# A transformer block on one core: weight parts spread over the heads, and a written order for VectorE and ScalarE in the FFN

## The chip, the cores and the metric

The kernel runs on one core of a Trainium2 chip. The metric is the device time of that core in microseconds (us), the median of several runs of the compiled program. The engines are called as in the profile: PE is TensorE, DVE is VectorE, ACT is ScalarE, POOL is GpSimd, and SP is SyncE, which issues the DMAs.

## The reference

For B=4 batches of S=512 tokens with D=256 features, everything in fp32:

```python
sa, ca, ga, sb, cb, gb = (silu(c) @ wmod).reshape(B, 6, 1, D) parts
ga, gb = sign * max(|g|, 0.25)
h = layernorm(x) * (1 + ca) + sa
x = x + ga * attention(h)          # 16 heads of 128, causal softmax, W_O
h = layernorm(x) * (1 + cb) + sb
x = x + gb * ffn(h)

def ffn(x):
    h = x @ down_w + down_b                      # 256 -> 128
    logits = x @ router_w + router_b - 1e-7 * cost
    top 2 of softmax(logits); gate = softmax of the two
    out = sum over the two of gate * expert(h * mask) summed over all 8 experts
          # expert: gelu(gelu(hm) @ w1 + b1) @ w2 + b2, hidden 128, 256, 384, 512 (twice)
    out += 0.1 * shared_expert(h)
    return out @ up_w + up_b + gelu(x) @ core_w + core_b
```

## The kernel before

**Products.** Each fp32 product is made of three products of rounded parts (`mm3`, lines 139 to 141): a matrix is split into hi (rounded, a copy on ACT or DVE) and lo (the rest, a subtraction in `rest`, line 147, on DVE or POOL).

**Heads.** The first loop runs over 64 heads: four groups of four heads, in each group over the batches. A head makes its scores (L475 is its first product, a diagonal block), the mask with the row maximum (DVE, L481, which gives `nmax`), the exponentials (ACT, L491), the row sums' reciprocals and a scaling (POOL, L496), a transpose through DRAM (`turned`, tile `aT`), the hi and lo parts of it, the product with the values (`mixed`, tile `pz`, parts `zh` and `zl`) and the product with W_O (`project_out`, tile `po`). At the last head of a batch the residual is added: `tmp` on DVE (L583), `x` on POOL (L585). The products with the values lag `LAG` heads behind.

**Weight units.** The FFN's weights are kept as units of up to 512 columns. Eleven of them (`TO_PART`: first0 to first4, second0 to second2, shared, core, down) are split during the heads by `part_wf`: a load into a buffer of tag "stage" (two buffers), a hi copy on ACT (L227), a store of it to DRAM, the subtraction on POOL, and a store of that. They are loaded again later into the buffers of the weights. Head number n splits the unit that `PART_AT` gives for it.

**FFN.** `all_ffn` runs over 4 batches and in each over 21 chunks of 128 hidden units (k = 0 to 20; the last is the shared expert). `first` makes the chunk's first product `ph` (from `ghh` and `ghl`, the parts of gelu(down)) and its gelu `hid` on ACT; where the chunk is not used whole, ACT and DVE then split it into `ah` and `al`. Three chunks later (`FFN_LAG`) `second` makes the product `acc`, DVE evicts an expert's sum into `part`, and POOL adds it to `oacc` (L856). `gelu_inputs`, called at k=10, makes gelu(x) and its parts for the core product (POOL adds h2F at L864, ACT's gelu, POOL's `gxh` and `gxl`); `core` at k=19 and 20 (`FFN_CORE`) makes that product and `outputs` of a batch comes at k=6 of the next. `output_bias` loads `out_b` and makes `obias` on POOL (L725) at k=12 of batch 0.

**Norm and routing.** The FFN of batch b needs its second layernorm and its routing. `normed` makes statistics on DVE (L346, L348), `rstd` on POOL (L350, L351: an addition and a power) and `xn` on DVE (L354); `modulated` transposes it on PE (`ptn`, L383), scales it, and splits it into `hTh` and `hTl`; `route` makes the router's product (`pl`, L610) and then a chain of short DVE operations on [32 x 128] tiles with three trips to ACT (L642 among them). `finish` enters these steps into `later` for two to eight steps after the batch's last head: for batch 0 and 1 these are still heads (batch 1's modulation and routing fall on heads 62 and 63), for batch 2 and 3 they lie among the chunks of batch 0 and 1, two or three chunks to a step.

**Order.** PE's instructions run in the order of the program from the start (`manual_schedule`, L150). The other engines' instructions are put in order by the scheduler, which works through a simulated timeline, takes the program's order as priority, and lets an instruction that is ready pass one that is not. Some are tied by `issue_after`.

Of the kernel before, what the change touches and what calls it, by code (L numbers as in the profile page):

```python
# [11 lines left out]
F32 = mybir.dt.float32  # L12
# [83 lines left out]
FFN_CORE = (19, 20)  # L96
BEFORE3 = 4
EARLY = 2

TO_PART = tuple(u for u, (_, in_parts) in UNITS.items() if in_parts)  # L100
PART_AT = (17, 19, *range(20, 28), 33)
# [11 lines left out]
def adaln_attention_moe_kernel(  # L113
# [103 lines left out]

    def part_wf(u: str):

        n = len(UNITS[u][0]) * P  # L220
        st = work.tile([P, 512], F32, tag="stage", name=f"st_wf_{u}")[:, :n]
        load_runs(st, wf_runs(u))
        d = parts_d[u] = dram.tile([P, 3, n], F32, tag=f"wfp_{u}", name=f"wfp_{u}")
        if u.startswith("second"):
            nc.sync.dma_start(d[:, 2, :], st)
        hi = work.tile([P, 512], F32R, tag="stage", name=f"hi_wf_{u}")[:, :n]
        nc.scalar.copy(hi, st)  # L227
        nc.sync.dma_start(d[:, 0, :], f32(hi))
        rest(nc.gpsimd, st.bitcast(F32R), st, hi)
        nc.sync.dma_start(d[:, 1, :], st)  # L230
# [110 lines left out]
    def normed(b: int, which: int):  # L341

        st = small.tile([P, NT, 6], F32, tag="st", name=f"st_{b}_{which}")
        mv = small.tile([P, NT, 2], F32, tag="mv", name=f"mv_{b}_{which}")
        for t in range(NT):
            nc.vector.bn_stats(st[:, t, :], xs[b][:, t, :])  # L346
        for t in range(NT):
            nc.vector.bn_aggr(mv[:, t, :], st[:, t, :])  # L348
        rstd = small.tile([P, NT], F32, tag="rstd", name=f"rstd_{b}_{which}")
        nc.gpsimd.tensor_scalar(rstd, mv[:, :, 1], LN_EPS, 1.0, ALU.add, ALU.mult)  # L350
        nc.gpsimd.tensor_tensor(rstd, rstd, minus_half, ALU.pow)  # L351
        xn = work.tile([P, DC, NT, P], F32, tag="xn", name=f"xn_{b}_{which}", bufs=1)
        for t in range(NT):
            nc.vector.tensor_scalar(  # L354
                xn[:, :, t, :],
                xs[b][:, t, :].rearrange("p (c d) -> p c d", c=DC),
                mv[:, t, 0:1],
                rstd[:, t : t + 1],
                ALU.subtract,
                ALU.mult,  # L360
            )
        return xn
# [8 lines left out]
    def modulated(b: int, which: int):  # L371


        xn = xns[b, which]
        hi = const.tile([P, DC, S], F32R, tag=f"hTh{b}", name=f"hTh_{b}_{which}")
        lo = const.tile([P, DC, S], F32R, tag=f"hTl{b}", name=f"hTl_{b}_{which}")
        (h2T if which else hT)[b] = hi, lo
        first = not (b or which)
        whole = []
        for c in range(DC):  # L380
            ptr = psum.tile([P, S], F32, tag="pj", name=f"ptn_{b}_{which}_{c}", bufs=3)
            for t in range(NT):
                nc.tensor.transpose(ptr[:, ts(t, P)], xn[:, c, t, :], ident)  # L383
            scale = modT[:, 4 * which + 2 + c, b : b + 1]
# [6 lines left out]
            whole.append(ptr)  # L391

            for d in (c,) if not first else range(DC) if c == DC - 1 else ():
                nc.scalar.copy(hi[:, d, :], whole[d])
                recent["norm"] = rest(nc.vector, lo[:, d, :], whole[d], hi[:, d, :]).ins
            yield
# [4 lines left out]

    def norm_batch(b: int, which: int):
        if which and b > 1:
            with tc.issue_after(recent["hidden"]):
                xns[b, which] = normed(b, which)
            return
        xns[b, which] = normed(b, which)
# [184 lines left out]
    def route(b: int):  # L592

        n = S // R
# [14 lines left out]
        for i, (c, a) in enumerate(parts):  # L609
            nc.tensor.matmul(  # L610
                pl, lhsT=rw[:, c], rhs=a[:, c, :], start=i == 0, stop=i == len(parts) - 1
            )
        lt = work.tile([P, S], F32, tag="stage", name=f"lt_{b}")[:R]
        nc.vector.transpose(lt, pl)
        lt3 = lt.rearrange("p (j e) -> p j e", e=R)
        lg = small.tile([P, n * E], F32, tag="r_lg", name=f"r_lg_{b}", bufs=1)[:R]
# [6 lines left out]
        nc.vector.tensor_tensor(lg, lg, row(rbias[:R]), ALU.add)  # L623
        m, sm, f, g1, g2 = (t2(nm) for nm in ("m", "sm", "f", "g1", "g2"))
        desc = rt[:R, R_DESC - R_ROUTER : R_DESC - R_ROUTER + E]

        def top(hot):


            nc.vector.tensor_reduce(m, lg, AX.X, ALU.max)  # L630
            nc.vector.tensor_tensor(lg, lg, each(m), ALU.subtract)
            nc.vector.scalar_tensor_tensor(s, lg, 0.0, row(desc), op0=ALU.is_ge, op1=ALU.mult)  # L632
            nc.vector.tensor_reduce(f, s, AX.X, ALU.max)
            nc.vector.tensor_tensor(hot, s, each(f), ALU.is_equal)

        def exp(to, a, spare):


            if b == 0:
                last_exps["route"] = nc.scalar.activation(to, a, AF.Exp).ins  # L640
                return
            nc.scalar.activation(to, a, AF.Tanh, scale=0.5)  # L642
            nc.vector.tensor_scalar(spare, to, -1.0, 1.0, ALU.mult, ALU.add)
# [3 lines left out]
        top(hot1)  # L647
        exp(ex, lg, gt)
# [3 lines left out]
        top(gt)  # L652


        exp(g1, m, g2)
        nc.vector.scalar_tensor_tensor(g1, g1, 1.0, sm, op0=ALU.subtract, op1=ALU.mult)
        nc.scalar.activation(g1, g1, AF.Tanh, scale=-0.5)
        nc.vector.tensor_scalar(g2, g1, -0.5, 0.5, ALU.mult, ALU.add)
        nc.vector.tensor_scalar(g1, g1, 0.5, 0.5, ALU.mult, ALU.add)
        nc.vector.tensor_tensor(hot1, hot1, each(g1), ALU.mult)  # L660
        nc.vector.tensor_tensor(gt, gt, each(g2), ALU.mult)

# [66 lines left out]

    def before_chunks(b: int):  # L730
# [18 lines left out]
    class Mixture:  # L749
# [23 lines left out]
        def first(self, k: int, at: int):  # L773
# [14 lines left out]
            if k in WHOLE or (not b and k < NCH):  # L788
                tag = "aTh" if b and WHOLE.index(k) % 3 == 2 else "qh"
                if not b:  # L790
                    tag = ("qh", "e")[k % 2]
                hid = work.tile([P, S], F32, tag=tag, name=f"hid_{b}_{k}")
                recent["hidden"] = nc.scalar.activation(
                    hid, ph, AF.Gelu, bias=bias
                ).ins
                return k, hid
            hid = work.tile([P, S], F32, tag="e", name=f"hid_{b}_{k}")
            nc.scalar.activation(hid, ph, AF.Gelu, bias=bias)
            self.parted += 1
# [3 lines left out]
            if e == E:  # L803
                nc.scalar.activation(ah, hid, AF.Copy, scale=0.1)
                nc.vector.scalar_tensor_tensor(
                    al, hid, 0.1, f32(ah), op0=ALU.mult, op1=ALU.subtract
                )
            else:
                recent["hidden"] = nc.scalar.copy(ah, hid).ins
                recent["parted"] = rest(nc.vector, al, hid, ah).ins  # L810
# [47 lines left out]
        def gelu_inputs(self):  # L858

            hh, hl = h2T[self.b]  # L860
            gxh, gxl = self.gx
            hF = work.tile([P, DC, S], F32, tag="T", name=f"h2F_{self.b}")
            for c in range(DC):
                nc.gpsimd.tensor_tensor(hF[:, c, :], f32(hh[:, c, :]), f32(hl[:, c, :]), ALU.add)  # L864
                nc.scalar.activation(hF[:, c, :], hF[:, c, :], AF.Gelu)
                nc.gpsimd.tensor_scalar(gxh[:, c, :], hF[:, c, :], 1.0, 1.0, ALU.mult, ALU.mult)
                rest(nc.gpsimd, gxl[:, c, :], hF[:, c, :], gxh[:, c, :])
# [53 lines left out]
    def all_ffn():  # L921
# [5 lines left out]
        for b in range(B):  # L927
            m = Mixture(b)
            for k in range(NCH + 1):
# [6 lines left out]
                going.append((m, *begun))  # L936
                at += 1
                if k == FFN_OUT and before:
                    before.outputs()
                if k == 10:  # L940
                    with tc.issue_after(recent["added"]):
                        m.gelu_inputs()
                if at == NCH + FFN_LAG:
# [6 lines left out]
                if b + 1 < B:  # L950
                    if k == 16:
                        prepared[b + 1] = before_chunks(b + 1)
                    if k in FFN_CORE:
                        m.core(len(m.pys))
# [39 lines left out]
    def finish(n: int, b: int, h: int, z):  # L994
        project_out(b, h, z)
        if h == H - 1:
            later.setdefault(n + 1, []).append((norm_batch, b, 1))
            later.setdefault(n + 3 + (b > 1) + (BEFORE3 - 1) * (b > 2), []).append((modulate, b, 1))
            later.setdefault(n + 4 + (b > 1) + (BEFORE3 - 1) * (b > 2), []).append((route, b))
# [21 lines left out]
    for n, (b, h) in enumerate(order):  # L1021
# [18 lines left out]
        for f, *args in later.pop(n, ()):  # L1040
            f(*args)
        if n in PART_AT:
# [42 lines left out]

    steps = all_ffn()
# [6 lines left out]
    while going:  # L1093
# [4 lines left out]
        end_norm()  # L1098
        if waiting:
            db, dh, aT = waiting.pop(0)  # L1100
            done.append((db, dh, mixed(db, dh, aT)))
        if n == N:
            with tc.issue_after(recent["z"]):
                part_one(-1)
# [84 lines left out]
```

## Time and profile before

| | us |
|---|---|
| median of 3 runs | 824.99 (823.43 to 825.74) |
| the profiled execution | 824.06 |
| its span, first to last instruction | 822.3 |
| PE busy in it | 777.1 (95%) |
| DVE, POOL, ACT busy | 597.4, 521.4, 490.4 |
| mean granted clock of PE | 0.988 |
| heads | about 20 to 625 |
| FFN chunks | about 625 to 822 |

The page's busy shares are averages over the heads and the FFN, which have different loads. A line of the timeline gives start, length, engine, line of the code, operation, output and inputs, and in brackets the idle time before it and what ended that. In a line of waits the columns are total, number and longest.

### The profile page before, as it was taken

The page shows a single profiled execution, that of the slowest core. Times are in us where ns is not written, and L with a number is a line of the kernel's source. Part 1 is how long each engine was busy: PE and PEld are TensorE (multiplying, and loading weights), DVE is VectorE, ACT ScalarE, POOL GpSimd, SP SyncE. Part 2 cuts the span into 40 slices and gives each one's busy share as a digit, 9 for nine tenths or more (in the row PEclk, how much of TensorE's full clock was granted, in tenths as well). Part 3 has the DMA queues.
Part 4 walks back from the last instruction along what each step waited for, and adds up shares of the span by engine and source line. Part 5 has one row for each costly group of instructions (what it writes and reads, how often), then busy time and mean ns, then how long its engine had stood idle before and what let it go on. Part 6 is the DMA issues. An engine that isn't in the chain of part 4 may idle for free. (4 is left out here: it accounts for less than half of the span.)

```text
span 822.3 us, 14105 instructions
## 1 busy us (share of the span) xinstructions
PE 777.1 (95%) x4487; PEld 671.3 (82%) x4487; DVE 597.4 (73%) x1734; ACT 490.4 (60%) x1184; POOL 521.4 (63%) x523
## 2 busy tenths in 40 slices
PE   6889999999998799999999999999998898989997
PEld 5678989999887689999999999999887775767775
DVE  5968787776655676767777776779898577795555
ACT  3556666566656656666666656665667343656663
POOL 4645566886756568866556895656565346564675
PEclk9999999999999999999999999999999899999999
DMA  7365354666676746665454665554566332222221
GB/s 235 113 182 156 111 151 128 198 174 204 200 212 198 218 151 183 188 179 161 128 156 133 198 168 162 165 157 138 155 182 216 104 120 86 94 62 68 61 81 61
DMA packets 73218, 124.12 MB, mean 151 GB/s; under 512 B 8996, under 2 KB 51252, under 8 KB 73144
## 3 DMA queue, kind: packets, MB, share of 16 engines
q1 hardware_dynamic: 73112, 123.21, 51.1%
q8 instruction: 36, 0.59, 0.3%
q14 instruction: 38, 0.31, 0.1%
q0 software_dynamic: 32, 0.02, 0.0%
HBM read 73.05 MB, written 50.14 MB: 150 GB/s over the span
## 5 line engine op out<-in xcount | busy, mean ns | idle before, releaser
L147 POOL TENSOR_TENSOR aT<-aT,aTh 128x1152 fp32r<-128x1152 f32 x64 | 171.9, 2687 | 127.1 <-ACT aTh L528 124.2
L496 POOL TENSOR_SCALAR e<-e,inv 128x128 f32<-128x128 f32 (+3 forms) x256 | 135.7, 543 | 66.8 <-DVE inv L495 64.8
L491 ACT ACTIVATE e<-e,nmax 128x128 f32<-128x128 f32 (+3 forms) x256 | 143.4, 562 | 45.9 <-DVE nmax L481 44.8
L528 ACT CAST aTh<-aT 128x1152 fp32r<-128x1152 f32 x64 | 74.0, 1156 | 127.4 <-DMA aT<-moved 64.5
L481 DVE CUSTOM_DVE_ANT_0 e<-ps,mask 128x128 f32<-128x128 f32 (+3 forms) x256 | 120.9, 479 | 31.0 <-PE ps L475 19.7
L511 DVE STREAM_TRANSPOSE T<-e 128x384 f32<-128x384 f32 (+2 forms) x256 | 100.4, 445 | 9.8 <-POOL e L496 9.7
L139 PE MATMUL ps<-kh,ql 128*128 128x256 f32 (+2 forms) x192 | 72.0, 375 | 17.1 <-DVE nmax L481 17.1
L147 DVE TENSOR_TENSOR zl<-pz,zh 128x512 fp32r<-128x512 f32 x64 | 44.0, 687 | 56.9 <-ACT zh L546 56.3
L139 PE MATMUL po<-wo,zl 128*128 128x256 f32 x256 | 73.3, 286 | 4.5 <-DVE zl L147 4.2
L140 PE MATMUL po<-wo,zh 128*128 128x256 f32 x256 | 72.0, 281 | 0.0
L141 PE MATMUL po<-wo,zh 128*128 128x256 f32 x256 | 72.0, 281 | 0.0
L139 PE MATMUL pv<-wv,hTl 128*128 128x256 f32 x256 | 71.7, 280 | 0.0
L140 PE MATMUL pv<-wv,hTh 128*128 128x256 f32 x256 | 71.5, 279 | 0.0
L141 PE MATMUL pv<-wv,hTh 128*128 128x256 f32 x256 | 71.5, 279 | 0.0
L856 POOL TENSOR_TENSOR oacc<-oacc,part 128x512 f32<-128x512 f32 x28 | 40.9, 1462 | 43.4 <-DVE part L852 36.8
L495 DVE RECIPROCAL inv<-tot 128x1 f32<-128x1 f32 x256 | 40.0, 157 | 36.5 <-ACT e L491 29.6
L139 PE MATMUL pz<-aTh,vl 128*128 128x512 f32 (+2 forms) x192 | 65.5, 341 | 0.0
L140 PE MATMUL pz<-aT,vh 128*128 128x512 f32 (+2 forms) x192 | 65.3, 340 | 0.0
L140 PE MATMUL ps<-kl,qh 128*128 128x256 f32 (+2 forms) x192 | 65.2, 339 | 0.2 <-DVE kl L147 0.2
L141 PE MATMUL pz<-aTh,vh 128*128 128x512 f32 (+2 forms) x192 | 65.3, 340 | 0.0
L141 PE MATMUL ps<-kh,qh 128*128 128x256 f32 (+2 forms) x192 | 64.9, 338 | 0.0
L139 PEld LDWEIGHTS ps<-kh,ql 128*128 128x128 f32 x192 | 36.6, 191 | 28.0 <-DVE nmax L481 19.9
(216 smaller groups left out, 2331.2 us busy)
## 6 DMA issues: line engine op xcount, KB each, us to landing
moved<-T SPq DMA_DIRECT2D x256, 160.0 KB, 2.8
aT<-moved SPq DMA_DIRECT2D x64, 640.0 KB, 3.9
spread<-gates_e SPq DMA_DIRECT2D x32, 256.0 KB, 3.2
st_wqk<-in_wqk SPq DMA_DIRECT2D x16, 256.0 KB, 3.8
wf_first<-wfp_first SPq DMA_DIRECT2D x5, 512.0 KB, 5.9
st_wv<-in_wv SPq DMA_DIRECT2D x8, 256.0 KB, 3.4
st_wo<-in_wo SPq DMA_DIRECT2D x8, 256.0 KB, 3.7
wmod<-in_wmod SPq DMA_DIRECT2D x6, 256.0 KB, 5.2
```

The source lines that it names most:

```text
L139: nc.tensor.matmul(o, lhsT=wl, rhs=mh, start=start, stop=False)
L140: nc.tensor.matmul(o, lhsT=wh, rhs=ml, start=False, stop=False)
L141: nc.tensor.matmul(o, lhsT=wh, rhs=mh, start=False, stop=stop)
L147: return eng.tensor_tensor(lo, full, f32(hi), ALU.subtract)
L481: least = nc.vector.tensor_tensor_reduce(out=et, in0=ps[:, :n], in1=maskf[:, S - n :], scale=-SCALE, scalar=BIG, op0=ALU.add, op1=ALU.min, ...
L491: exp = nc.scalar.activation(et, et, AF.Exp, bias=nm[:, t : t + 1], scale=-1.0, accum_out=tot[:, t : t + 1])
L495: nc.vector.reciprocal(inv[:, one], tot[:, one])
L496: by_sum = nc.gpsimd.tensor_scalar(et, et, inv[:, one], 1.0, ALU.mult, ALU.mult)
L511: nc.vector.transpose(to[:, first : first + n], blocks[:, at : at + (n - 1) * step + 1 : step])
L528: nc.scalar.copy(hi, full)
L856: recent["added"] = nc.gpsimd.tensor_tensor(oacc, oacc, to, ALU.add).ins
```

## The change

**Units.** `part_wf` is cut in two: `stage_wf` allocates the buffer and issues the load, in the program one head before the split. `PART_AT` goes from consecutive heads to every second one in three groups.

**Core and gelu.** `FFN_CORE` goes from (19, 20) of the batch itself to (4, 5) of the next one. `gelu_inputs` is cut: POOL's adds come at k=9, and `gelu_parts` (ACT's gelu, POOL's two parts) at k=11 and 12, one half each; before, all came at k=10.

**Order.** From the last head on, DVE and ACT too run in the order of the program. The split of a chunk's hidden units (`parts`) stands after the older chunk's second product.

**Pieces.** `normed`, `modulated` (for batch 1 on) and `route` are cut by `yield` into pieces. The second norms of batch 2 and 3, and the modulation and routing of batch 1, 2 and 3, are entered into one list, `beside`, and `next_piece` issues the next piece behind each chunk's parts: two for a chunk of batch 0 or one that is used whole, one otherwise. So batch 1's modulation and routing move from heads 62 and 63 to the first chunks of batch 0. The split of the last head's weights (`part_one(-1)`) moves one step later.

```diff
-FFN_CORE = (19, 20)
+FFN_CORE = (4, 5)
-PART_AT = (17, 19, *range(20, 28), 33)
+PART_AT = (7, 9, 11, 20, 22, 24, 26, 36, 38, 40, 42)
...
+    def stage_wf(u: str):
+        n = len(UNITS[u][0]) * P
+        staged[u] = work.tile([P, 512], F32, tag="stage", name=f"st_wf_{u}")[:, :n]
+        load_runs(staged[u], wf_runs(u))
+
     def part_wf(u: str):
         n = len(UNITS[u][0]) * P
-        st = work.tile([P, 512], F32, tag="stage", name=f"st_wf_{u}")[:, :n]
-        load_runs(st, wf_runs(u))
+        st = staged[u]
...
         nc.gpsimd.tensor_tensor(rstd, rstd, minus_half, ALU.pow)
-        xn = work.tile([P, DC, NT, P], F32, tag="xn", name=f"xn_{b}_{which}", bufs=1)
+        for _ in range(3):
+            yield
+        xn = xns[b, which] = work.tile([P, DC, NT, P], F32, tag="xn", name=f"xn_{b}_{which}", bufs=1)
...
+        if which and b:
+            for c in range(DC):
+                turn(c)
+                yield
+                scaled(c)
+                yield
+                parts(c)
+            yield
+            return
...
+    beside: list = []
+
+    def next_piece():
+        while beside:
+            if next(beside[0], True) is None:
+                return
+            beside.pop(0)
...
-                going.append((m, *begun))
+                going.append((m, *m.parts(*begun)))
+                for _ in range(2 if k in WHOLE or not b else 1):
+                    next_piece()
                 at += 1
+                if before and k in FFN_CORE:
+                    before.core(len(before.pys))
                 if k == FFN_OUT and before:
                     before.outputs()
-                if k == 10:
+                if k == 9:
                     with tc.issue_after(recent["added"]):
                         m.gelu_inputs()
+                if k in (11, 12):
+                    m.gelu_parts(k - 11)
...
-                    if k in FFN_CORE:
-                        m.core(len(m.pys))
...
-        if h == H - 1:
+        if h < H - 1:
+            return
+        if b < 2:
             later.setdefault(n + 1, []).append((norm_batch, b, 1))
-            later.setdefault(n + 3 + (b > 1) + (BEFORE3 - 1) * (b > 2), []).append((modulate, b, 1))
-            later.setdefault(n + 4 + (b > 1) + (BEFORE3 - 1) * (b > 2), []).append((route, b))
+        if b == 0:
+            later.setdefault(n + 3, []).append((modulate, b, 1))
+            later.setdefault(n + 4, []).append((all_of, route, b))
+        else:
+            if b > 1:
+                beside.append(normed(b, 1))
+
+            beside.extend((modulated(b, 1), route(b)))
...
+        if n + 1 in PART_AT:
+            stage_wf(TO_PART[PART_AT.index(n + 1)])
         if n in PART_AT:
             part_wf(TO_PART[PART_AT.index(n)])
...
+    ctx.enter_context(
+        tc.manual_schedule(engines={mybir.EngineType.DVE, mybir.EngineType.Activation})
+    )
     steps = all_ffn()
...
+        if n == N + 1:
+            with tc.issue_after(recent["z"]):
+                part_one(-1)
         if waiting:
             db, dh, aT = waiting.pop(0)
             done.append((db, dh, mixed(db, dh, aT)))
-        if n == N:
-            with tc.issue_after(recent["z"]):
-                part_one(-1)
```

More of the change, by code (lines that the diff above doesn't have):

```diff
@@ L216, in wf_runs @@
         return [wf[:, at * P : (at + n) * P] for at, n in runs(UNITS[u][0])]
+    staged: dict[str, bass.AP] = {}
+    def stage_wf(u: str):
+        n = len(UNITS[u][0]) * P
+        staged[u] = work.tile([P, 512], F32, tag="stage", name=f"st_wf_{u}")[:, :n]
+        load_runs(staged[u], wf_runs(u))
     def part_wf(u: str):
         n = len(UNITS[u][0]) * P
-        st = work.tile([P, 512], F32, tag="stage", name=f"st_wf_{u}")[:, :n]
-        load_runs(st, wf_runs(u))
+        st = staged[u]
         d = parts_d[u] = dram.tile([P, 3, n], F32, tag=f"wfp_{u}", name=f"wfp_{u}")
@@ L346, in normed @@
             nc.vector.bn_stats(st[:, t, :], xs[b][:, t, :])
+            if t % 2:
+                yield
         for t in range(NT):
@@ L361, in normed @@
             )
-        return xn
+            if t % 2:
+                yield
     recent: dict[str, mybir.Instruction] = {}
@@ L379, in modulated, with turn @@
         whole = []
-        for c in range(DC):
+        def turn(c: int):
             ptr = psum.tile([P, S], F32, tag="pj", name=f"ptn_{b}_{which}_{c}", bufs=3)
@@ L383, in modulated, with scaled @@
                 nc.tensor.transpose(ptr[:, ts(t, P)], xn[:, c, t, :], ident)
+            whole.append(ptr)
+        def scaled(c: int):
+            ptr = whole[c]
             scale = modT[:, 4 * which + 2 + c, b : b + 1]
@@ L390, in modulated, with parts @@
                 nc.vector.tensor_scalar(ptr, ptr, scale, shift, ALU.mult, ALU.add)
-            whole.append(ptr)
+        def parts(c: int):
+            nc.scalar.copy(hi[:, c, :], whole[c])
+            recent["norm"] = rest(nc.vector, lo[:, c, :], whole[c], hi[:, c, :]).ins
+        if which and b:
[3 more added lines that the diff above has]
+                scaled(c)
+                yield
+                parts(c)
+            yield
+            return
+        for c in range(DC):
+            turn(c)
+            scaled(c)
             for d in (c,) if not first else range(DC) if c == DC - 1 else ():
-                nc.scalar.copy(hi[:, d, :], whole[d])
-                recent["norm"] = rest(nc.vector, lo[:, d, :], whole[d], hi[:, d, :]).ins
+                parts(d)
             yield
@@ L400, in adaln_attention_moe_kernel, with all_of @@
     vs: dict[tuple[int, int], tuple] = {}
+    def all_of(f, *args):
+        for _ in f(*args):
+            pass
     def norm_batch(b: int, which: int):
[L403 to L407, printed above, removed]
+        all_of(normed, b, which)
     def gate_attention(b: int):
@@ L612, in route @@
             )
+        yield
         lt = work.tile([P, S], F32, tag="stage", name=f"lt_{b}")[:R]
@@ L615, in route @@
         lt3 = lt.rearrange("p (j e) -> p j e", e=R)
+        yield
         lg = small.tile([P, n * E], F32, tag="r_lg", name=f"r_lg_{b}", bufs=1)[:R]
@@ L623, in route @@
         nc.vector.tensor_tensor(lg, lg, row(rbias[:R]), ALU.add)
+        yield
         m, sm, f, g1, g2 = (t2(nm) for nm in ("m", "sm", "f", "g1", "g2"))
@@ L631, in top @@
             nc.vector.tensor_tensor(lg, lg, each(m), ALU.subtract)
+            yield
             nc.vector.scalar_tensor_tensor(s, lg, 0.0, row(desc), op0=ALU.is_ge, op1=ALU.mult)
@@ L642, in exp @@
             nc.scalar.activation(to, a, AF.Tanh, scale=0.5)
+            yield
             nc.vector.tensor_scalar(spare, to, -1.0, 1.0, ALU.mult, ALU.add)
@@ L645, in exp @@
             nc.vector.scalar_tensor_tensor(to, to, 1.0, spare, op0=ALU.add, op1=ALU.mult)
-        top(hot1)
-        exp(ex, lg, gt)
+        yield from top(hot1)
+        yield
+        yield from exp(ex, lg, gt)
+        yield
         nc.vector.tensor_reduce(sm, ex, AX.X, ALU.add)
@@ L651, in route @@
         nc.vector.scalar_tensor_tensor(lg, hot1, -BIG, lg, op0=ALU.mult, op1=ALU.add)
-        top(gt)
-        exp(g1, m, g2)
+        yield
+        yield from top(gt)
+        yield
+        yield from exp(g1, m, g2)
         nc.vector.scalar_tensor_tensor(g1, g1, 1.0, sm, op0=ALU.subtract, op1=ALU.mult)
+        yield
         nc.scalar.activation(g1, g1, AF.Tanh, scale=-0.5)
+        yield
         nc.vector.tensor_scalar(g2, g1, -0.5, 0.5, ALU.mult, ALU.add)
@@ L661, in route @@
         nc.vector.tensor_tensor(gt, gt, each(g2), ALU.mult)
+        yield
         ge = s.rearrange("p j e -> p (j e)")
@@ L792, in first @@
                 hid = work.tile([P, S], F32, tag=tag, name=f"hid_{b}_{k}")
-                recent["hidden"] = nc.scalar.activation(
-                    hid, ph, AF.Gelu, bias=bias
-                ).ins
+                nc.scalar.activation(hid, ph, AF.Gelu, bias=bias)
                 return k, hid
@@ L798, in first, with parts @@
             nc.scalar.activation(hid, ph, AF.Gelu, bias=bias)
+            return k, hid
+        def parts(self, k: int, hid):
+            b, e = self.b, self.order[k][0]
+            if k in WHOLE or (not b and k < NCH):
+                return k, hid
             self.parted += 1
@@ L808, in first @@
             else:
-                recent["hidden"] = nc.scalar.copy(ah, hid).ins
-                recent["parted"] = rest(nc.vector, al, hid, ah).ins
+                nc.scalar.copy(ah, hid)
+                rest(nc.vector, al, hid, ah)
             return k, (ah, al)
@@ L860, in gelu_inputs, with gelu_parts @@
             hh, hl = h2T[self.b]
-            gxh, gxl = self.gx
[L862 to L867, printed above, removed]
+            self.hF = work.tile([P, DC, S], F32, tag="T", name=f"h2F_{self.b}")
+            for c in range(DC):
+                nc.gpsimd.tensor_tensor(
+                    self.hF[:, c, :], f32(hh[:, c, :]), f32(hl[:, c, :]), ALU.add
+                )
+        def gelu_parts(self, c: int):
+            gxh, gxl = self.gx
+            hF = self.hF[:, c, :]
+            nc.scalar.activation(hF, hF, AF.Gelu)
+            nc.gpsimd.tensor_scalar(gxh[:, c, :], hF, 1.0, 1.0, ALU.mult, ALU.mult)
+            rest(nc.gpsimd, gxl[:, c, :], hF, gxh[:, c, :])
         def gate_bias(self, obias):
@@ L1084, in adaln_attention_moe_kernel @@
                     load_wf(u)
+    ctx.enter_context(
+        tc.manual_schedule(engines={mybir.EngineType.DVE, mybir.EngineType.Activation})
+    )
     steps = all_ffn()
```

## The prediction

> **What bounds the kernel now.** I read the page first, then PE's list of waits, then windows over the span, and last the timelines of the stretches where PE is not full.
>
> ```profile
> PE 777.1 (95%) x4487; PEld 671.3 (82%) x4487; DVE 597.4 (73%) x1734; ACT 490.4 (60%) x1184; POOL 521.4 (63%) x523
> PEclk9999999999999999999999999999999899999999
> ```
>
> PE is busy 95% of the span; nothing else is near. The change adds and removes no product, so all that it can move is the 822.3 - 777.1 = 45.2 us in which PE idles, and the time at a lower clock. PE's waits, by what ended them:
>
> ```profile
> PE ps L139 <- DVE nmax L481: 17.1, 13, 3.2
> PE pt_mod L298 <- DVE sc L257: 6.4, 1, 6.4
> PE po L139 <- DVE zl L147: 4.2, 2, 2.2
> PE acc L139 <- ACT ah L809: 3.1, 1, 3.1
> PE ph L139 <- ACT hid L793: 2.7, 2, 2.1
> PE ph L140 <- DVE ghl L147: 1.9, 1, 1.9
> PE ph L139 <- DVE ghh L741: 0.9, 1, 0.9
> ```
>
> The columns are total, times, longest. The 6.4 is the start and stays. Where the others lie, by windows (length, then PE, PEld, DVE, ACT, POOL busy, clock):
>
> ```profile
> 200.00:220.00 20.00, 20.00 (x126) 17.94 (x125) 13.41 (x43) 12.04 (x32) 15.96 (x17) 1.00 0.66 208
> 220.00:260.00 40.00, 32.82 (x199) 28.45 (x198) 22.25 (x74) 19.86 (x52) 22.21 (x22) 1.00 0.69 209
> 260.00:300.00 40.00, 35.38 (x223) 31.70 (x222) 24.35 (x79) 25.67 (x67) 23.16 (x24) 1.00 0.64 194
> 620.00:640.00 20.00, 15.29 (x93) 12.67 (x91) 16.55 (x43) 14.02 (x28) 13.95 (x11) 0.98 0.55 175
> 640.00:660.00 20.00, 19.23 (x95) 16.08 (x96) 9.57 (x37) 6.67 (x11) 3.87 (x3) 0.85 0.37 107
> 720.00:740.00 20.00, 16.91 (x71) 12.42 (x69) 18.30 (x36) 11.13 (x20) 13.42 (x10) 0.91 0.20 59
> ```
>
> Three stretches lose time: heads 20 to 28 (211-309 us), the passage from heads to chunks (625-646), and places in batches 0 and 1. A head that waits for nothing takes 9.19 us from its first score product to the next head's; heads 20 to 28 exceed this by 0.25, 1.80, 0.91, 3.96, 2.35, 1.47, 3.41, 0 and 1.14, together 15.3. The reason stands in ACT's timeline:
>
> ```profile
> 185.38 0.63 ACT L227 CAST hi_wf_first<-st_wf_first 128x512 fp32r<-128x512 f32 x1
> 248.53 0.62 ACT L227 CAST hi_wf_second<-st_wf_second 128x512 fp32r<-128x512 f32 x1 [5.98 <-DMA st_wf_second<-in_wf]
> ```
>
> The rounding copy of a unit (L227) sits in ACT's queue before the exponentials. Units alone in a head find their load landed (185.38); in consecutive heads the two "stage" buffers are not free in time, ACT idles up to 5.98 us on the load, the head's exponentials, their sums and finally PE stand behind it.
>
> **Part 1, units loaded one head early and spread out.** The work is the same: 11 copies of 0.41-0.63 us on ACT, 11 subtractions on POOL, the same loads and stores on SP. In the order of the two built programs the move is smaller than the diff says: the scheduler still puts each load and copy as early as a "stage" buffer allows. The copies land in heads 2, 3, 4 (first0-2), then at four neighbouring places from head 19 to 21 (first3, first4, second0, second1), then at four from 35 to 37 (second2, shared, core, down). The first three enter heads that already exceed 9.19 by 1.4-2.0, where DVE is late; bounds -2 to +4, taken as 0, since ACT has slack there. Prices for the two groups of four come from the heads above: first in a run 0.25, second 1.80, third 0.91, fourth the median of what followed, about 1.47 (0 to 3.96): 4.4 for the first group. The second has smaller units (128x256 for two) and one real wait, core's load, whose row of before is 3.41: 3.4. So 15.3 - 4.4 - 3.4 = 7.5 saved, bounds -1 to 13. SP issues the eight spread loads earlier, past the transfers of the attention weights; DMA share is 0.64-0.69 in these windows, the same as in the full 200-220, so I cost that at nothing; uncovered, it is one more late load (3 us).
>
> **Part 2, the passage from heads to chunks.** Batch 1's modulation and routing leave heads 62 and 63 and become pieces behind batch 0's chunks. Before, PE waited 0.72 (scores), 0.88 (ghh), 1.91 (ghl), 1.96 (zl) from 627 to 639, and then ran at half clock from 639.1 to 645.9; in the window 639 to 646 PE is busy 5.23 us at clock 0.51, and half of that, 2.6, is lost: 8.07 in all. In the new order ghh and ghl follow directly on the last residual's products, with no routing in front. Left over are 0.4-0.5 before the first chunk, some 0.5 elsewhere, and a new wait: batch 1's router product (pl) stands right behind chunk 2's first product and waits for the lo part of its input, about 1.4. 8.07 - 2.5 = 5.5 saved (3 to 7).
>
> **Part 3, batch 0, chunk 13: a new wait.** This is where I expect the change to give time back. Batch 2's norm is now pieces; its xn needs rstd from POOL, and PE's transpose of xn (ptn) stands behind chunk 13's first product. What POOL did here before:
>
> ```profile
> 669.37 0.73 POOL L725 TENSOR_TENSOR obias<-out_b 128x256 f32<-128x256 f32 x1 [2.50 <-DMA out_b<-in_rows]
> 670.19 0.19 POOL L350 TENSOR_SCALAR rstd<-mv 128x4 f32<-128x4 f32 x1
> 670.47 1.02 POOL L351 TENSOR_TENSOR rstd<-rstd,minus_half 128x4 f32<-128x4 f32 x1
> 671.46 1.27 POOL L856 TENSOR_TENSOR oacc<-oacc,part 128x512 f32<-128x512 f32 x1
> 676.39 2.56 POOL L864 TENSOR_TENSOR h2F<-hTh,hTl 128x512 f32<-128x512 f32 x2
> 679.04 0.62 POOL L866 TENSOR_SCALAR gxh<-h2F 128x512 fp32r<-128x512 f32 x1
> ```
>
> In the new POOL order gelu's adds (moved from k=10 to 9), a sum, two roundings and a subtraction stand before the power: obias, oacc, h2F twice, oacc, gxh, rstd's first step, gxh, gxl, then the power. From the last po product (662.56 in this trace, called 0): obias ends at 669.37 + 0.73 - 662.56 = 7.5; oacc 8.8; two h2F 11.35; oacc 12.6; gxh 13.25; rstd 13.45; gxh 14.1; gxl (1.33 in the trace) 15.4; power 16.4; four xn on DVE (2.0-2.3) 18.4. PE comes to ptn after the 1.5 of po and its chunks of 1.45 each: at 10.7. The stall is 18.4 - 10.7 = 7.7 us (5.3 if the load of out_b does not bind, 8.5 with one more sum ahead). While xn waits, DVE's fixed order holds chunk 6's part and the scaling of ptn behind it; ACT's holds later gelus. After the 3.09 us gap at 723.6 this trace shows half clock from 727.9 to 731.3, 1.7 lost; a gap of over twice that loses 1.7-3.4, taken as 2.6. A wait for the router product of batch 2 at chunk 15 adds 0.7. Together 11.0, against 2.94 (2.10 + 0.62 + 0.23) that batch 0's later chunks lost before: 8 given back, between -3 and +12.
>
> [...]
>
> **Part 4, batch 1 and the rest.** The 3.09 wait of acc at 726.70 is ACT standing behind a routing tanh that waits for DVE, and it cost 1.7 more at half clock: 4.8. In the written order each part of a chunk comes before a routing piece, so it goes; in its place I put 1.0 for batch 3's routing product. DVE is busy 18.30 of 20 there, and gets some 3 us more norm work, which two core pieces on PE (2 us each, moved from k=19, 20 to 4, 5 of the next batch) leave room for. 3.8 saved (-1 to 4.8). Batches 2 and 3 and the tail (0.73) keep their waits. The core products move past no waiting load; the outputs still come at k=6, two chunks behind them.
>
> **Sum.** -7.5 - 5.5 + 8.0 - 3.8 = -8.8. The profiled execution took 824.06 (span 822.3 and 1.8 around it), so 815.3; the median of the runs is 0.93 higher: 816.2.
>
> **Rivals.** (a) *Chunk 13 does not stall* (rstd gets its turn on POOL before gelu's parts bind): part 3 gives 0, the sum is -16.8, about 808 (805-811). For it: the releases on POOL depend on ACT and DMA ends that I took from before. Against: the built order has eight POOL instructions ahead of the power.
> (b) *Slower: the fixed order on DVE and ACT.* Before, a late result was stepped around; now all behind it waits. Each routing has two or three trips DVE-ACT-DVE, three routings and two norms lie among the chunks of batches 0 and 1, and the trace's price of one such blocked trip is 3.09 + 1.7 = 4.8. Chunk 13 at its 12, batch 1's gain lost, and two more such blocks: -7.5 - 5.5 + 12 + 9.6 = +8.6, about 834; one block, 829. It decides once the fixed order's waits in the chunks pass 16.8 us, the sum of the gains of parts 1, 2 and 4. Against: parts come before pieces in the written order.
> (c) *The units are not spread.* The copies still come one behind the other, four and four; if each run costs what the old one did, part 1 gives 0 and the sum is -1.3, about 823.5. For it: same two buffers, same hoisting.
>
> **How the numbers follow.** Forecast 0.45 (own range 810-822), (a) 0.24, (b) 0.17, (c) 0.14. 0.3% is 2.5 us, about what a measurement of this kernel can tell from no change. The forecast and (a) lie below 822.5, and a third of (c): faster 0.74; most of the rest of (c) same, 0.08; (b) and a bit of (c) slower, 0.18. The range reaches from (a)'s lower end, 805, to (b)'s single block, 829.
>
> **What would show it.** Right: the ACT waits for unit loads in heads 20-28 gone or halved, PE full in 300-340 of the old count, a PE wait ptn <- DVE xn of 5 to 9 us in batch 0, no wait acc <- ah near 3 us, no 0.9 and 1.9 on ghh and ghl. Wrong: heads 35-37 or 2-4 each over 3 us late, no wait at ptn, or several PE waits of 2-4 us on ACT or DVE among the chunks of batch 0 and 1.

## The result, and the profile after

The changed kernel takes 825.68 us (median of 12 runs, 823.43 to 826.86) against 824.46 us of the kernel before beside it (12 runs): a ratio of 1.0017, interval 1.0000 to 1.0034. Within the 2.5 us that count as no change, the time is the same; the forecast gain of 8.8 us is not there. The profiled execution took 825.62 us, with a span of 823.9.

Page, the engines' line and the clock row:

```profile
PE 778.5 (94%) x4487; PEld 669.3 (81%) x4487; DVE 591.2 (72%) x1734; ACT 489.3 (59%) x1184; POOL 521.4 (63%) x523
PEclk9999999999999999999999999999999989999999
```

PE's list of waits (total, times, longest). The line numbers are those of the changed kernel: L140 to L142 are the three products, L513 is the mask, L523 the exponential, L365 `xn`, L910 the eviction into `part`:

```profile
PE ps L140 <- DVE nmax L513: 13.2, 12, 2.8
PE ptn L396 <- DVE xn L365: 5.7, 1, 5.7
PE acc L141 <- DVE al L148: 4.0, 3, 2.1
PE acc L140 <- DVE part L910: 2.2, 2, 1.3
PE acc L886 <- DVE part L910: 0.8, 1, 0.8
```

The waits for ghh, ghl, zl, hid and ah of before are gone, and `ps <- nmax` fell from 17.1 to 13.2. In their place stand one wait of 5.7 for `xn` and six of together 7.0 on DVE's `al` and `part`. By windows (length, then PE, PEld, DVE, ACT, POOL busy, clock, DMA share, GB/s):

```profile
220.00:260.00 40.00, 38.07 (x234) 33.50 (x233) 27.35 (x89) 24.48 (x65) 23.98 (x24) 1.00 0.67 202
260.00:300.00 40.00, 40.00 (x254) 36.55 (x254) 29.02 (x94) 25.84 (x67) 25.95 (x27) 1.00 0.54 151
360.00:400.00 40.00, 38.19 (x236) 33.83 (x234) 25.20 (x85) 22.96 (x63) 23.62 (x25) 1.00 0.65 194
```

```profile
617.89:653.00 35.11, 31.43 (x166) 24.90 (x165) 19.26 (x50) 18.23 (x31) 13.95 (x12) 0.95 0.42 130
653.00:690.18 37.18, 31.17 (x122) 20.74 (x121) 23.30 (x59) 12.47 (x22) 21.37 (x20) 0.91 0.36 111
690.18:736.34 46.16, 40.80 (x177) 29.09 (x176) 40.26 (x81) 25.76 (x44) 24.56 (x19) 1.00 0.22 66
736.34:775.69 39.35, 37.42 (x157) 27.34 (x156) 25.40 (x38) 24.50 (x40) 25.60 (x19) 1.00 0.27 73
```

The heads are nearly full now (38.07 and 40.00 where 32.82 and 35.38 stood). The FFN is not. Its four windows begin at the last head's first score product (617.89; before 625.63), at about the last W_O products (653.0; 661.35), and at about the starts of batches 1 and 2 (690.18 and 736.34; 696.73 and 741.04); the fourth ends where batch 3 starts (775.69; 777.54). Counting in each PE's gaps, and half of its busy time in stretches at half clock:

| stretch | before: idle + clock | after: idle + clock | difference | forecast |
|---|---|---|---|---|
| start of the last head | 625.63 | 617.89 | -7.7 | -7.5 |
| last head to last W_O product | 5.47 + 2.58 | 3.68 + 1.70 | -2.7 | -5.5 |
| rest of batch 0 | 2.94 + 0 | 6.01 + 2.85 | +5.9 | +8.0 |
| batch 1 | 3.09 + 1.71 | 5.35 + 0 | +0.6 | -3.8 |
| batch 2 | 0 | 1.92 + 0 | +1.9 | 0 |

These sum to -2.0, while the span grew by 1.6. Of the 3.6 between, 0.9 are batch 1's transposes, which left head 62 for the chunks, and 0.3 a longer tail behind the last product. The other 2.4 lie in PE's busy time in the chunks (counted from one product's start to the next, `pl` takes 1.2 us more in all, `ph` 1.5, half clock included); what makes them is not shown.

POOL's timeline at batch 0's chunk 13, the `xn` that waits for it on DVE, and the product that waits for `xn` on PE:

```profile
660.05 0.78 POOL L770 TENSOR_TENSOR obias<-out_b 128x256 f32<-128x256 f32 x1 [2.32 <-DMA out_b<-in_rows]
...
662.03 2.50 POOL L921 TENSOR_TENSOR h2F<-hTh,hTl 128x512 f32<-128x512 f32 x2
...
668.50 1.02 POOL L360 TENSOR_TENSOR rstd<-rstd,minus_half 128x4 f32<-128x4 f32 x1
```

```profile
669.55 2.32 DVE L365 TENSOR_SCALAR xn<-x,mv,rstd 128x256 f32<-128x256 f32 x4 [6.47 <-POOL rstd L360]
```

```profile
670.96 0.47 PE L396 MATMUL ptn<-ident,xn 128*128 128x128 f32 x1 [5.70 <-DVE xn L365]
```

That is the chain of the prediction, in its order. What it did not have is in ACT's timeline from 724 to 739, at the end of batch 1 and the start of batch 2, in three places:

```profile
724.22 0.31 ACT L679 ACTIVATE lt<-r_lg 32x128 f32<-32x128 f32 x1 [2.27 <-DVE r_lg L667]
...
733.04 0.21 ACT L679 ACTIVATE r_g<-r_m 32x16 f32<-32x16 f32 x1 [3.35 <-DVE r_m L666]
...
738.40 0.21 ACT L700 ACTIVATE r_g<-r_g 32x16 f32<-32x16 f32 x1 [3.92 <-DVE r_g L698]
```

A routing tanh of 0.2 to 0.3 us holds ACT for up to 3.92 us while DVE works off its own queue; the gelu and the hi copy of the next chunks stand behind it, and `al` and `part` on DVE after them. Five of the six waits for `al` and `part` lie from 722 to 743, around these places. Two have no late tanh in front of them: at 0.87, the first of the five, `part` stands on DVE behind the routing's own steps, and at 1.43, the sixth (702.24), DVE is at the last steps of batch 2's routing and the constants of `cvec` (L756 to L761).

### The profile page after: what moved, and what is told of

It reads as the page before. It is cut to its first block, busy times and chain, and to the rows that moved or that the text cites. A ratio compares the mean times of both kernels' runs of the same rounds, so it can differ in the third digit from the quotient of the medians.

```text
span 823.9 us, 14100 instructions
## 1 busy us (share of the span) xinstructions
PE 778.5 (94%) x4487; PEld 669.3 (81%) x4487; DVE 591.2 (72%) x1734; ACT 489.3 (59%) x1184; POOL 521.4 (63%) x523
## 5 line engine op out<-in xcount | busy, mean ns | idle before, releaser
L523 ACT ACTIVATE e<-e,nmax 128x128 f32<-128x128 f32 (+3 forms) x256 | 143.4, 562 | 51.8 <-DVE nmax L513 51.0
L513 DVE CUSTOM_DVE_ANT_0 e<-ps,mask 128x128 f32<-128x128 f32 (+3 forms) x256 | 120.2, 477 | 27.4 <-PE ps L507 17.2
L140 PE MATMUL ps<-kh,ql 128*128 128x256 f32 (+2 forms) x192 | 71.6, 373 | 13.2 <-DVE nmax L513 13.2
L140 PE MATMUL po<-wo,zl 128*128 128x256 f32 x256 | 73.0, 285 | 0.0
L140 PE MATMUL pv<-wv,hTl 128*128 128x256 f32 x256 | 72.0, 281 | 0.6 <-DVE hTl L148 0.6
L142 PE MATMUL pv<-wv,hTh 128*128 128x256 f32 x256 | 71.5, 279 | 0.0
L142 PE MATMUL po<-wo,zh 128*128 128x256 f32 x256 | 71.5, 279 | 0.0
L142 PE MATMUL ps<-kh,qh 128*128 128x256 f32 (+2 forms) x192 | 65.0, 338 | 0.0
L140 PE MATMUL pz<-aTh,vl 128*128 128x512 f32 (+2 forms) x192 | 64.9, 338 | 0.0
L142 PE MATMUL pz<-aTh,vh 128*128 128x512 f32 (+2 forms) x192 | 64.9, 338 | 0.0
L140 PEld LDWEIGHTS ps<-kh,ql 128*128 128x128 f32 x192 | 36.5, 190 | 23.8 <-DVE nmax L513 16.6
```

The source lines that it names most:

```text
L140: nc.tensor.matmul(o, lhsT=wl, rhs=mh, start=start, stop=False)
L142: nc.tensor.matmul(o, lhsT=wh, rhs=mh, start=False, stop=stop)
L513: least = nc.vector.tensor_tensor_reduce(out=et, in0=ps[:, :n], in1=maskf[:, S - n :], scale=-SCALE, scalar=BIG, op0=ALU.add, op1=ALU.min, ...
L523: exp = nc.scalar.activation(et, et, AF.Exp, bias=nm[:, t : t + 1], scale=-1.0, accum_out=tot[:, t : t + 1])
```

## The experiments

Theory A was: the units gave the heads what was forecast, and in the chunks the written order of DVE and ACT turns late results into new PE waits, at chunk 13 through POOL's queue and in batches 1 and 2 through the routing pieces. All times are medians of the runs; ratios are to the kernel before in the same batch of runs, with a 95% interval.

**The units alone.** The kernel before with

```diff
-PART_AT = (17, 19, *range(20, 28), 33)
+PART_AT = (7, 9, 11, 20, 22, 24, 26, 36, 38, 40, 42)
...
+        if n + 1 in PART_AT:
+            stage_wf(TO_PART[PART_AT.index(n + 1)])
```

> The kernel before with the units' edit alone (stage_wf one head early, the new PART_AT); everything from the last head on as before. Theory A (the heads' part of the sum held, the chunks took it back): heads 20 to 63 gain 7 to 8 us as they did in the changed kernel (19.9 to 617.9 there, 19.7 to 625.6 before), nothing else moves: 816 to 818 us. Rival B (the shorter heads come from batch 1's modulation and routing leaving heads 62 and 63, not from the units): 0 to 3 us gained, 821 to 824.

Measured 817.72 us, ratio 0.9903 (0.9875 to 0.9930). In its profile the last head starts at 619.62, 6.0 before the old one, and its FFN keeps the old waits (1.01 ghh, 1.90 ghl, 2.03 zl, 2.10 hid, 3.09 ah). From there to the end the two profiles take the same, 196.7. B falls: the heads' gain belongs to the units.

**Everything but the units.** The changed kernel with that edit undone:

```diff
-PART_AT = (7, 9, 11, 20, 22, 24, 26, 36, 38, 40, 42)
+PART_AT = (17, 19, *range(20, 28), 33)
...
-        st = staged[u]
+        st = work.tile([P, 512], F32, tag="stage", name=f"st_wf_{u}")[:, :n]
+        load_runs(st, wf_runs(u))
```

> The changed kernel with the old PART_AT and the load inside the split; the written order, the pieces, the core and gelu moves stay. Theory A: it loses what the units gave, 7 to 8 us: 832 to 834, slower than before by 8 to 10 us. Rival B (units worth little): 826 to 829.

Measured 832.83 us, ratio 1.0083 (1.0053 to 1.0114). Within the noise, the change is the sum of two parts that cancel: -8.0 from the units and +7.2 from all the rest. In this profile the last head starts 1.6 later than before (2.5 lost in heads 3 to 5, 0.9 won where the transposes left head 62), and the time from there to the end is 204.5 in place of 196.7.

**POOL's order at chunk 13.** The changed kernel with

```diff
-                if k == 9:
+                if k == (9 if b else 14):
                     with tc.issue_after(recent["added"]):
                         m.gelu_inputs()
-                if k in (11, 12):
-                    m.gelu_parts(k - 11)
+                first_part = 11 if b else 16
+                if k in (first_part, first_part + 1):
+                    m.gelu_parts(k - first_part)
```

> The changed kernel with batch 0's gelu adds at chunk 14 and its parts at 16 and 17, so that on POOL the power of batch 2's rstd stands in front of them; the other batches unchanged. Theory A (POOL's order makes the 5.70 us wait of ptn and the half clock after it, 2.85): the wait shrinks below 1 us, no half clock near 670: 816.5 to 819. Rival C (the load of out_b and the statistics on DVE are late too, the next cause is right behind): 2 to 5 us of the wait stay, 820 to 823.

Measured 822.09 us, ratio 0.9946 (0.9921 to 0.9971): 3.6 us below the changed kernel's 825.68, which is of other runs; A expected 7 to 9. The wait for `xn` did fall to 0.97 and the half clock near 670 went, 7.6 us together. PE's list of waits shows what took its place:

```profile
PE acc L140 <- ACT hid L849: 2.0, 1, 2.0
...
PE ptn L396 <- DVE xn L365: 1.0, 1, 1.0
```

The 2.0 is at 690.63, behind two routing tanhs (687.80 and 691.62) for which ACT had waited 1.82 and 0.91 on DVE. Half clock from 732.7 to 736.1, 1.7 lost, follows the wait of 2.05 for `al`, which the changed kernel has too, there without half clock. So C's number came out, but not for C's reason: no load or statistic was late; routing pieces, the second place of theory A, took 2.0 of the time won, and the clock 1.7.

**The scheduler's order again.** The changed kernel without

```diff
-    ctx.enter_context(
-        tc.manual_schedule(engines={mybir.EngineType.DVE, mybir.EngineType.Activation})
-    )
     steps = all_ffn()
```

> The changed kernel without the written order of DVE and ACT from the last head on: the scheduler orders them again; pieces, units, core and gelu moves stay. Theory A (in batches 1 and 2 ACT stands behind routing tanhs in the written order): the waits of acc on al and part in batches 1 and 2, 7.3 us, go down to 3 or less; chunk 13's wait may stay: 817 to 822. Rival D (DVE is simply full there, 18.5 of 20 us, in any order): the waits stay within 2 us of 7.3: 824 to 827.

Measured 815.93 us, ratio 0.9877 (0.9854 to 0.9901), better than expected. The waits in batches 1 and 2 are 0.92, 0.14, 1.21 and 0.09, together 2.4 in place of 7.3: D falls. In this run DVE is busy 19.76 of 20 us from 714 to 734, fuller than in the changed kernel (18.53 from 720 to 740), and ACT still idles 2.97 and 2.33 us in front of two tanhs, but the gelus that PE needs next were made ahead of them:

```profile
PE pl L643 <- DVE hTl L148: 4.0, 1, 4.0
...
PE acc L141 <- DVE al L148: 1.2, 1, 1.2
PE acc L140 <- ACT hid L849: 0.9, 1, 0.9
```

Chunk 13's wait went too, since the scheduler puts the power on POOL in front of gelu's parts; a new one of 4.02 came two chunks later, at `pl <- hTl`.

**The early down product.** The changed kernel with batch 0's down product moved up (`down` is that product, taken out of `before_chunks`):

```diff
         if nb is not None:
             q = project(nb, nh, 0)
+        else:
+            pd0 = down(0)
...
-            prepared[0] = before_chunks(0)
+            prepared[0] = before_chunks(0, pd0)
```

> The changed kernel with batch 0's down product (pd, six products, some 1.4 us at full clock) issued between the last head's second and third score products, where PE waits 2.51 us and then runs at half clock from 622 to 626 (1.7 lost). Theory A (PE comes there too early since batch 1's router products left, and DVE's mask comes 0.86 later): the wait falls by the pd's time to about 1.1, no half clock: 3 us less, 822 to 823.5. Rival E (the mask only moves along, or PE then waits for ghh, ghl or zl instead): 0 to 1 us less, 824.5 to 826.

Measured 825.25 us, ratio 0.9996 (0.9978 to 1.0015). The wait for the mask fell from 2.51 to 1.00, as A said, but PE then waits 1.50 for ghh, which the program ties behind the last exponential, and the half clock only moves (631 to 635). E holds: the wait moved on to the next late result.

**Batch 3's routing kept for batch 2.**

```diff
-    def next_piece():
-        while beside:
+    def next_piece(keep: int = 0):
+        while len(beside) > keep:
...
-                    next_piece()
+                    next_piece(1 if b == 1 else 0)
```

> The changed kernel with batch 3's routing pieces kept back until batch 2's chunks; the order stays written. Theory A (ACT and DVE stand behind the routing pieces in batch 1): the waits from 720 to 742 of the changed kernel (0.87, 0.83, 2.05, 0.52, 1.30, with some 0.2 behind each) go, batch 2, which has no other pieces, gets 1 to 3 us of them: 3 to 5 us less, 821 to 823. Rival F (any chunk with a routing piece loses the same, wherever it stands): no change, 825 to 827.

Measured 821.30 us, ratio 0.9951 (0.9933 to 0.9969). PE's waits for `acc`:

```profile
PE acc L141 <- DVE al L148: 4.0, 2, 2.5
PE acc L140 <- DVE part L910: 0.2, 1, 0.2
```

The waits from 722 to 742 shrink to 0.17. What is left of `al` is the 1.43 at chunk 4 of batch 1, and one of 2.52 in batch 2. So it is the routing pieces that hold PE there. Among batch 2's chunks they cost less, 2.52; why is not shown.

**Scheduler's order and early down product together.** The edits of the early down product and of the scheduler's order, both in the changed kernel.

> The scheduler's order of DVE and ACT in the chunks, as in the run without the written order, and the early down product. Theory A: the two gains add: 815.9 less 3, 812 to 814. Rival E: 815 to 817.

Measured 813.60 us, ratio 0.9857 (0.9836 to 0.9878), in A's range; the interval overlaps that of 815.93, so the 2.3 us between are not settled.

**Order edges for the pieces.** The kernel of the last experiment, with

```diff
                 for _ in range(2 if k in WHOLE or not b else 1):
-                    next_piece()
+                    with tc.issue_after(recent["norm"]):
+                        next_piece()
```

> As the last, with each piece's DVE instructions kept behind the latest lo part of a modulation (an order edge), so that batch 3's xn no longer passes batch 2's hTl on DVE. In the run without the written order that xn took 4.74 us and PE's router product of batch 2 waited 4.02 for hTl, with half clock from 673 to 681. Theory A: wait and half clock go: 5 to 7 us below the last kernel, 806 to 808. Rival G (batch 3's norm is missed later or the statistics crowd another chunk): 2 us or less below it.

Measured 812.76 us, ratio 0.9840 (0.9818 to 0.9861). The 4.0 at `pl` fell to 0.31 and the half clock behind it went, but a wait of 2.60 for `zl` and half clock from 645 to 649 came. That is G's number, 2 us or less below the last kernel, by another cause than G's. `zl` stood on DVE behind a routing step that lasted as long as POOL's subtraction beside it. DVE's timeline, then POOL's:

```profile
640.36 2.55 DVE L681 TENSOR_SCALAR lt<-lt 32x128 f32<-32x128 f32 x1 [1.01 <-ACT lt L679]
```

```profile
640.20 2.63 POOL L148 TENSOR_TENSOR aT<-aT,aTh 128x1152 fp32r<-128x1152 f32 x1 [3.27 <-ACT aTh L560]
```

**Both single remedies in the written order.** The edits at chunk 13 and of the kept routing, together, in the changed kernel.

> The changed kernel, order still written, with both single remedies: batch 0's gelu behind the power on POOL, and batch 3's routing kept for batch 2. Alone they gave 3.6 and 4.4 us. Theory A (two separate places where the written order lets a late result hold PE): they add, 816.5 to 819. Rival C (each remedy pushes its POOL or DVE work into the other's place): 820 to 822.

Measured 816.79 us, ratio 0.9915 (0.9891 to 0.9939): 7.2 us below the kernel before of its runs (824.02), where the two alone gave 3.6 and 4.4. In the profiles, the time from the last head's start to the end is 8.8 below the changed kernel's, with the two alone 5.3 and 4.1. They nearly add, so they are two places.

**POOL's gelu out of the way.** The kernel with the scheduler's order and the early down product, with batch 0's gelu and gate bias later:

```diff
-                if k == 9:
+                if k == (9 if b else 16):
...
+                first_part = 11 if b else 18
...
-                if k == (3 if b else 14):
+                if k == (3 if b else 19):
```

> The kernel with the scheduler's order and the early down product, with batch 0's gelu (adds at chunk 16, parts at 18 and 19) and gate bias (19) taken from POOL during chunks 11 to 15. DVE's order around batch 2's hTl and batch 3's xn is unchanged. There the four xn took 4.74 us beside POOL's subtractions and additions, and PE waited 4.0 with half clock after it. Theory H (DVE's operations are held by POOL's): the four xn take 1.4 to 3 us, the wait falls to 2 or less, the half clock goes: 809 to 811. Rival I (xn is slow by itself, or waits for its own inputs): the four keep over 4 us and the time stays at 813 to 814.

Measured 813.27 us, ratio 0.9874 (0.9849 to 0.9899). Batch 3's `xn` on DVE, first in the kernel without these edits, beside POOL's work for gelu, then here (the order on DVE is the same), and the one POOL operation that still lies beside it here:

```profile
666.23 4.72 DVE L365 TENSOR_SCALAR xn<-x,mv,rstd 128x256 f32<-128x256 f32 x4
```

```profile
667.61 2.03 DVE L365 TENSOR_SCALAR xn<-x,mv,rstd 128x256 f32<-128x256 f32 x4
```

```profile
667.24 1.28 POOL L918 TENSOR_TENSOR oacc<-oacc,part 128x512 f32<-128x512 f32 x1 [0.90 <-DVE part L914]
```

One by one, the four take 1.46, 1.35, 1.35 and 0.81 in the first and 1.06, 0.40, 0.40 and 0.40 in the second.

The wait at `pl` fell from 4.0 to 1.31, and the half clock there went. H holds for the four `xn`, 2.03 in place of 4.72, and misses the time: beside POOL's work, now at chunks 16 to 19, DVE's small steps take up to 1.34, and PE waits later for 1.38 (`ph <- hid`), 0.78 and 0.96 (`acc <- al`).

The best kernel that was run is that with the order edges, 812.76 us, 1.6% below the kernel before. It, the one with POOL's gelu moved and the one with neither (813.6) can't be told apart.

**The runs side by side.** The time from the last head's first score product to the end, by the profiles, leaves out what the heads differ by: 196.7 before, 206.0 changed, 196.3 with the scheduler's order, 194.4 with the early down product too. So in these profiles the written order cost 9.7 us. In the scheduler's order, the pieces and the other moves alone gained little: 196.3 against 196.7, with batch 1's transposes (0.9) now in it.

## Why the prediction was wrong

**Part 1, right.** Forecast -7.5; the last head starts 7.7 us earlier, of which 0.9 are batch 1's transposes, and the units alone gave 8.0 in the median (6.0 between the two profiles). By heads, the early group cost nothing on balance, the second lost 3.3 in heads 22 to 24 (forecast 4.4), the third 3.9 in heads 37, 38 and 40 (forecast 3.4). A copy's price, taken from the old heads by its place in a run, held, though the fourth copy's should have been 1.9, the median of the six heads that it was taken from, and not 1.47. The copies do still come four and four, and some still wait for their load:

```profile
212.05 0.62 ACT L234 CAST hi_wf_first<-st_wf_first 128x512 fp32r<-128x512 f32 x1 [2.92 <-DMA st_wf_first<-in_wf]
...
364.40 0.41 ACT L234 CAST hi_wf_shared<-st_wf_shared 128x256 fp32r<-128x256 f32 x1 [4.96 <-DMA st_wf_shared<-in_wf]
```

**Part 2, half.** Forecast -5.5, measured -2.7. The waits for ghh, ghl and zl went as forecast and the new wait for `pl` was 1.1 in two pieces. The term "0.4-0.5 before the first chunk" was 2.51 plus 1.7 of half clock:

```profile
621.14 0.44 PE L140 MATMUL ps<-kh,ql 128*128 128x384 f32 x1 [2.50 <-DVE nmax L513]
```

I had expected no more at this product than its old 0.72. Before, four `pl` products of batch 1 (626.21 to 627.29) stood on PE in front of it; they left with the routing, so PE came 0.92 earlier in the head (0.74 after its start, 1.66 before). DVE's mask came 0.86 later in it (2.92 against 2.06), behind transposes that waited for POOL. 0.72 + 0.92 + 0.86 is 2.50. Work that is moved away from PE can be the cover of a wait that stays.

**Part 3, right in kind, mis-sized.** Forecast a 7.7 us wait and 2.6 of clock; measured 5.70 and 2.85. POOL ended the power 17.0 after the last W_O product started (16.4 forecast), but PE reached the transpose at 12.8, not 10.7, so that term of mine was short: some 1.4 of PE's way are the `pc` products (L748), which my sum left out. The experiment at chunk 13 shows POOL's order as the cause.

**Part 4, wrong.** Forecast -3.8, measured +0.6, and batch 2, forecast at 0, lost 1.9: 6.3 of the 10 us that I missed. The step that failed reads "In the written order each part of a chunk comes before a routing piece, so it goes". It holds for the parts of the same chunk alone. The next chunk's gelu stands behind the piece's tanh on ACT, the tanh behind DVE's queue, and the next `al` and `part` on DVE behind that gelu and the routing steps between. Undoing the order took 4.9 us off these waits; keeping batch 3's routing out of batch 1 took 3.0 off those of both batches. DVE's queue is long there also through steps that lie beside POOL's: from 720 to 738 seven of the routing's small steps take 7.9 us together, each beside a POOL operation, where steps of the same forms without one take about 1.7. The run with the scheduler's order has such rows too (up to 1.39), so they alone do not hold PE; no run takes them away in the written order.

**The rivals.** (b) named this mechanism and priced it, one blocked trip at 4.8; at 829 to 834 it overshot, since chunk 13 cost less than its 12 and the blocks in batches 1 and 2 were spread over six shorter waits without half clock. The measured 825.7 lies between the forecast and (b), and inside the range. (a) is wrong, chunk 13 stalls. (c) gives a time near the measured one, 823.5, by luck: the copies do come four and four, but their two runs cost 3.3 and 3.9, together less than half of the old 15.3.

**The clock.** The forecast let the gap at chunk 13 cost 2.6 of clock, an estimate from the drop of before after 3.09 us, which lost 1.7; it cost 2.85. In the trace after, PE dropped to half clock after 2.51 us (621.9 to 625.6, clock 0.54) and after 5.70 (669.9 to 676.7, clock 0.50), in the run of the early down product after gaps of 1.00 and 1.50 with products between, but not after the 2.05 at 733 nor, before, after 3.15. The same wait of 2.05, in the run of chunk 13's remedy, was followed by half clock. So the length of a gap alone did not decide it in these runs. In the traces of before and after, all changes of the clock, from the start of the first half clock to the start of the last, lie whole multiples of 3.413 us apart (before: 38.37, 639.12, 727.86; after: 38.37, 622.05, 669.84). I cut the two traces, from 17.9 us on, into steps of this length that start at those times. In eight steps at full clock PE idles for 1.96 us or more, and half clock follows on each of them; with 1.51 to 1.81 it follows on one of seven, with less on none. The 3.15 of before lies in two steps, 1.61 and 1.54. The 2.05 lies within one step where half clock came (729.32 to 732.73), and across two where it did not (731.28 to 734.69 has 1.44 of it).

## What to carry to other kernels

A written order takes away the scheduler's freedom to step around a late result; before writing one, follow for each small cross-engine step (a tanh, a power) who stands behind it on each engine's queue, POOL's and ACT's included, not only whether its chunk's own work comes first. Test the parts of a change alone: here -8 and +7 made "no change", and the good half was ready to keep. And when work moves off the bounding engine, look at which wait it had been covering.

## What the runs showed of the hardware that I had not expected

In these runs some short DVE operations took longer beside a POOL operation, one of them about as long as that operation. A 32x128 TENSOR_SCALAR that takes 0.21 us with POOL idle (two in the trace after) took 2.55 beside a POOL subtraction of 2.63, in the run with the order edges. An `xn` takes about 0.40 where no POOL operation lies beside it; the four took 4.72 beside POOL's work and 2.03 with only one addition of 1.28 beside the first, in the same order on DVE. In the trace after, 32x128 TENSOR_TENSOR on DVE takes 0.28 on average where POOL is idle (23 of them) and 0.70 where it overlaps (13, up to 1.34). What holds DVE there is not shown. DVE's busy share counts these longer times too, and the edit that moved POOL's gelu shortened the four `xn`.
